# A causal mask moved from the matrix engine to zeros written by GpSimd, with a reworked residual and last gates

## The chip, the cores and the metric

The kernel runs on one core of a Trainium2 chip. Its engines work side by side, each through its own instructions in order: TensorE (PE in the profile, with PEld for its weight loads), VectorE (DVE), ScalarE (ACT), GpSimd (POOL) and SyncE (SP), which here issues the DMAs. The metric is device time in microseconds; less is better. Numbers such as 1847.95 us are medians of several runs; the profile is one further execution, recorded instruction by instruction.

## What is computed

The input is `x` with 16 sequences ("batches" below) of 512 tokens of 128 channels. Four blocks follow one another, each with `x = layernorm(x + block(x))`:

```
block 1  x = ln(x)*ln0_g + ln0_b                          # so x enters the block's own residual
         xn = ln(x)*pre_g + pre_b; xx = xn one token earlier
         k = exp(min(mix_k(xn,xx) @ Wk, 60)); v = mix_v @ Wv; r = mix_r @ Wr
         wk, wkv = recurrences over the 512 tokens of k and k*v with decay and first
         x = x + (sigmoid(r) * wkv/(wk+eps)) @ Wo
         xn = ln(x)*post_g + post_b; x = x + sigmoid(mix @ cWr) + silu(mix @ cWk) @ cWv
block 2  a tree of 255 sigmoid gates gives 256 leaf probabilities, times leaf values, times Wout
block 3  16 heads of 8 channels, rotary positions;
         scores = q k^T / sqrt(8) + causal mask; out = softmax(scores) @ v @ Wo
block 4  softmax over 16 experts, the two greatest kept as gates g[e];
         u + sum over e of g[e]*(u @ Wr[e] + br[e]) + mean of two shared experts
```

## The kernel before

Everything of a batch is held as 128 channels on the partitions by 512 tokens. For each batch `front` (line 574) does blocks 1 and 2 and the queries and keys of block 3; its four `rwkv` pieces (line 625) do the recurrence in four chunks of 128 hidden channels. The attention runs in four groups of four heads. It makes two passes over the scores. In the first, `greatest` (line 854), the scores of 128 queries stand on the partitions (`sc`), a matmul with the mask's values adds -1e30 where a key lies in the future, and VectorE takes the greatest of each row (`nmx`). These maxima are appended to the queries as further rows by a small DMA (`rows`). In the second, `weighted` (line 910), 128 keys stand on the partitions (`st`); the maxima are then subtracted by the matmul itself, ScalarE takes the exponential into a tile `e` (`ew` in the profile), and `sums` (line 940) multiplies by the values with a column of ones (`vaug`), giving the weighted sum and the denominator (`o`). `ends` (line 956) divides, multiplies by Wo and normalizes to `u`. `gating` (line 1007) computes the gates, writes them to DRAM (`gd`) and reads each pair back, spread over all partitions (`gb`, 512 KB). `by_gate` (line 1080) multiplies `u` by one gate (`us`), and `experts` (line 1094) sums 16 matmuls of `us` and one of the shared experts into `acc`.

In the second pass a group has four key tiles. Tile `kt` holds keys 128 kt to 128 kt + 127 and only the queries from 128 kt on: 512, 384, 256 and 128 of them. Only the first 128 of these queries can lie before a key, so only these columns need the mask. Before, one more matmul per score tile, with weights `mask` and the moving operand `idents` (four copies of the identity), adds the mask to them.

The residual of block 1 keeps `x1` without its mean and bias. Each time it is needed, PE recomputes it: `centre` times `x1`, plus `b0p` times `ones`, which adds the centred bias `ln0_b` in three bf16 parts.

The order of the work is made by a planner that runs when the program is built (`Plan`, line 66). Each piece of work is a Python generator that yields when it must wait for an event, a slot or an engine. The planner keeps a clock for each engine with an estimated cost for each operation, and lets the piece with the smallest due time plus slack go first when an engine is free. Slacks are set by kind of work and engine (`S_FRONT` and the others, lines 46 to 53). `PERIOD` and `LEAD` set from when in the planner's time the next batch's front may start. `SCORES` bounds the score tiles in flight, over both passes; `BANKS` are the eight PSUM banks. Slots such as `e_slots` (two places for `e`), `gb_slots` (two for gates), `us_slots` (three) and `norms` (one) hold a piece until a place is free. What the planner decides is fixed: each engine's order in the program is the order in which the pieces issued. On the chip an engine waits only for the data and places of its own next instruction.

`V` and `W` both are VectorE; `W` marks operations for which the planner adds cost when GpSimd is busy. Nearly all instructions are issued through the helper at lines 216 to 224, so the profile shows line L219 for them, and they are told apart by the names of their tiles.

Of the kernel before, what the change touches and what calls it, by code (L numbers as in the profile page):

```python
# [17 lines left out]
NT = T // 128  # L18
# [24 lines left out]
SCORES = 5  # L43
PERIOD = 100.0

S_FRONT = {"PE": -6.0, "V": -6.0, "A": 0.0, "G": -20.0}
S_RWKV = {"PE": -10.0, "V": 15.0, "A": -10.0, "G": 6.0}
S_GREATEST = {"PE": -30.0, "V": -3.0, "A": -3.0, "G": -30.0}
S_WEIGHTED = {"PE": -20.0, "A": 30.0, "G": -15.0}
S_SUMS = {"PE": 15.0}  # L50
S_ENDS = {"PE": 6.0, "V": -6.0, "A": 50.0, "G": -15.0}
S_GATE = {"PE": -20.0, "V": 6.0, "A": 6.0, "G": 0.0}
S_EXPERTS = {"PE": 20.0}
FREE = {}
LEAD = 60.0
RWKV_PACE = 5.0
EXPERT_PACE = 0.0
# [151 lines left out]
class Engine:  # L209
# [5 lines left out]
    def __getattr__(self, op):  # L215
        def issue(out, *args, **kw):
            if self.name in self.plan.last:
                with self.plan.tc.issue_after(self.plan.last[self.name].ins):
                    ins = getattr(self.engine, op)(out, *args, **kw)  # L219
            else:  # L220
                ins = getattr(self.engine, op)(out, *args, **kw)
            self.plan.did(self.name, self.cost(op, out, *args))
            self.plan.last[self.name] = ins
            return ins
        return issue
# [27 lines left out]
def pool_us(op, out, *_):  # L253
    return 0.25 + 0.0022 * columns(out)
# [3 lines left out]
def rwkv_tree_attn_moe(ctx: ExitStack, tc: tile.TileContext, a: dict, out: bass.AP):  # L258
# [35 lines left out]
    e_slots, us_slots, gb_slots = Slots(plan, 2), Slots(plan, 3), Slots(plan, 2)  # L294
# [28 lines left out]
    w_at = load("w_at", pool=p2, tag="e4")  # L323
# [44 lines left out]
    ones, b0p, minus = fixed("ones", [PARTS, T], BF16), fixed("b0p", [PARTS, D], BF16), fixed("minus", [128, 2])  # L368
    decay, first = fixed("decay", [128, NC4]), fixed("first", [128, NC4])

    def prepare_mixes():

        V.memset(ones, 1.0)
        b0 = pp.tile([128, PARTS], F32, tag="b0", name="b0")
        for i in range(PARTS):
            V.tensor_copy(b0[:, i:i + 1], col(V_LN0B))
        yield
        p = yield from bank("p_b0")
        mm(p[0:PARTS, 0:D], b0, centre, start=True, stop=True)
# [8 lines left out]
        b0r = pp.tile([PARTS, D], F32, tag="b0r", name="b0r")  # L388
        V.tensor_copy(b0r, p[0:PARTS, 0:D])
        give(p)  # L390
        b0m = pp.tile([PARTS, D], BF16, tag="b0m", name="b0m")
        for i in range(PARTS):
            V.tensor_copy(b0m, b0r)
            V.tensor_tensor(b0r, b0r, b0m, ALU.subtract)
            if i == 0:
                V.tensor_scalar(b0p, b0m, ident[0:PARTS, 0:1], None, ALU.mult)
            else:
                V.scalar_tensor_tensor(b0p, b0m, ident[0:PARTS, i:i + 1], b0p, ALU.mult, ALU.add)
# [48 lines left out]
    masks, idents = (fixed(x, [128, HG, 128], BF16) for x in ("masks", "idents"))  # L447
    mask, identb = masks[:, 0, :], idents[:, 0, :]
# [7 lines left out]
    def prepare_attention():  # L456
# [12 lines left out]
        for i in range(HG):  # L469
            copy(masks[:, i, :], mask32)  # L470
            copy(idents[:, i, :], ident)
# [85 lines left out]
    def variance(d, tag):  # L557

        sq = t512(tag)
        act(sq, d, AF.Square)  # L560
# [13 lines left out]
    def front(b, keep):  # L574
# [19 lines left out]
        def shifted_norm(p, g, minus_b, b):  # L594

            r = yield from normed(p, sq, rr)
# [3 lines left out]
            V.scalar_tensor_tensor(xn[:, 1:T + 1], p, g, r, ALU.mult, ALU.mult)  # L600
            give(p)
# [14 lines left out]
        mm(p, centre, x1, start=True, stop=False)  # L616
        mm(p, b0p, ones, start=False, stop=True)
        yield
        dx, xx, shift = yield from shifted_norm(p, col(V_PREG), minus[:, 0:1], col(V_PREB))
# [54 lines left out]
        mm(p, centre, x1, start=True, stop=False)  # L674
        mm(p, b0p, ones, start=False, stop=False)
        event("x1", b).set()
        for c in range(NC4):
            yield event("rw", b, c)
            mm(p, tm_o[:, c, :], rw[:, c, :], start=False, stop=(c == NC4 - 1))
# [510 lines left out]
```

## Time and profile before

| | us |
|---|---|
| median of 3 runs | 1847.95 (1846.07 to 1852.24) |
| the profiled execution, whole | 1852.02 |
| its span, first to last instruction | 1850.2 |

| engine | first exponential and before it | rest |
|---|---|---|
| ACT, first `ew` of the second pass | starts at 203.5 | last starts at 1784.5 |
| SP, output of the first batch | issued at 450.58 | last at 1846.98 |

Times in the profile are from the span's start. A row such as "113.4, 221" after a group's form and count gives its busy time in us and the mean length of one in ns; what follows is the idle time of the engine just before these instructions and what ended it. "out<-in" names the tile written and those read. In a table by stretches, each engine's busy time in us stands with the number of its instructions, and behind them the granted TensorE clock (1.00 is full), the busy share of the DMA engines and their GB/s. Matmuls on PE are pipelined, and each fp32 matmul of 512 columns shows as two records.

### The profile page before, as it was taken

The numbers are of one execution on the slowest core, as the hardware profiler recorded it, in microseconds if no ns is written. First come the engines' busy times: TensorE is split into PE (matmuls) and PEld (weight loads), VectorE is DVE, ScalarE is ACT, GpSimd is POOL, SyncE is SP. The second block draws the span as 40 slices with busy tenths as digits, with TensorE's granted clock in tenths as the row PEclk, the third lists the DMA queues.
The fourth block names the chain that finished last, engine by engine and source line by source line (L and its number), as shares of the span: only waits on it lengthen the run. The fifth ranks groups of instructions, "written<-read, shape, count | busy, mean of one in ns | idle before, by whom it ended". The sixth has DMA issues, their size and how long they took to land.

```text
span 1850.2 us, 25410 instructions
## 1 busy us (share of the span) xinstructions
PE 1667.9 (90%) x8580; PEld 784.5 (42%) x8668; DVE 1367.0 (74%) x1917; ACT 1172.0 (63%) x1974; POOL 1063.3 (57%) x1329
## 2 busy tenths in 40 slices
PE   5577889899999999899999999999899999998875
PEld 2233434344444444444444444444344444454431
DVE  7695879688888778686887788796878868555512
ACT  3345677668677576667767676767667666765440
POOL 2344544556765747566565757675666757545342
PEclk9687999899999999999999999999999999999996
DMA  3001010221413122222313132222213131233322
GB/s 103 1 6 56 20 38 27 79 79 32 132 37 112 62 91 78 66 82 73 97 46 105 62 96 78 95 67 65 74 58 116 51 107 62 61 94 111 97 80 97
DMA packets 61970, 133.78 MB, mean 72 GB/s; under 512 B 11708, under 2 KB 32974, under 8 KB 61585
## 3 DMA queue, kind: packets, MB, share of 16 engines
q1 hardware_dynamic: 61841, 132.16, 22.6%
q8 instruction: 69, 1.13, 0.2%
q14 instruction: 60, 0.49, 0.1%
HBM read 114.01 MB, written 17.31 MB: 71 GB/s over the span
## 4 chain that ended last, share of the span: by engine, by line
PE 49%; DVE 25%; POOL 11%; issue 6%; ACT 4%; DMA 2%; SPq 1%; POOLq 0%; DVEq 0%; ACTq 0%
PE acc L219 8%; PE sc L219 7%; PE st L219 6%; DVE sk L219 6%; PE o L219 5%; DVE skv L219 5%; PE p L219 5%; PE pv L219 4%; DVE nmx L219 3%; PE pr L219 2%; PE ph L219 2%; POOL us L219 2%; PE pk L219 2%; POOL lp L219 2%; PE pvv L219 2%
## 5 line engine op out<-in xcount | busy, mean ns | idle before, releaser
L219 DVE TENSOR_REDUCE nmx<-sc 128x1 f32<-128x384 f32 (+3 forms) x704 | 433.8, 634 | 195.6 <-PE sc L219 148.4
L219 ACT ACTIVATE ew<-st 128x512 f32<-128x512 f32 (+1 forms) x704 | 382.3, 556 | 252.1 <-PE st L219 248.0
L219 POOL TENSOR_TENSOR us<-u,gb 128x512 f32<-128x512 f32 x248 | 328.5, 1334 | 159.3 <-PE acc L219 83.6
L219 PE MATMUL acc<-us,w_mo 128*128 128x512 f32 x512 | 277.7, 634 | 17.0 <-POOL us L219 16.7
L219 PE MATMUL st<-qop,kop 128*128 128x512 bf16 (+1 forms) x1018 | 253.9, 304 | 18.1 <-DMA qop<-rows 8.5
L219 PE MATMUL sc<-kop,qop 128*128 128x128 bf16 x1021 | 257.4, 305 | 11.3 <-DVE nmx L219 7.5
L219 DVE RECIPROCAL sk<-sk 128x512 f32<-128x512 f32 x64 | 213.8, 3341 | 0.0
L219 PE MATMUL o<-ew,vaug 128*32 128x512 f32 (+3 forms) x2048 | 193.8, 447 | 6.6 <-ACT ew L219 3.4
L219 POOL TENSOR_TENSOR sk<-fk,sk 128x512 f32<-128x512 f32 x64 | 102.2, 1597 | 142.2 <-DVE sk L219 123.3
L219 PEld LDWEIGHTS <-qop 128*128 128x128 bf16 x1024 | 94.1, 100 | 182.8 <-issue 158.7
L219 PE MATMUL st<-idents,masks 128*128 128x128 bf16 (+2 forms) x673 | 161.7, 240 | 0.6 <-issue 0.4
L219 PE MATMUL sc<-masks,idents 128*128 128x128 bf16 (+2 forms) x656 | 154.9, 236 | 0.3 <-issue 0.2
L219 PEld LDWEIGHTS <-kop 128*128 128x128 bf16 x1024 | 91.6, 99 | 146.7 <-issue 102.5
L219 POOL TENSOR_TENSOR skv<-t,skv 128x512 f32<-128x512 f32 x64 | 81.4, 1272 | 89.1 <-DVE skv L219 84.3
L219 POOL TENSOR_TENSOR rw<-skv,sk 128x512 f32<-128x512 f32 x64 | 86.8, 1357 | 64.5 <-DVE sk L219 61.0
L219 PEld LDWEIGHTS acc<-us,w_mo 128*128 128x128 f32 x512 | 84.1, 195 | 80.7 <-issue 42.1
L219 POOL TENSOR_TENSOR lp<-gates,lp 128x8 f32<-128x8 f32 (+6 forms) x224 | 115.2, 536 | 2.7
L219 DVE TENSOR_TENSOR_SCAN skv<-decay,kv 128x511 f32<-128x511 f32 x64 | 112.7, 1761 | 0.0
L219 PEld LDWEIGHTS <-idents 128*128 128x128 bf16 x704 | 69.8, 99 | 88.8 <-issue 82.9
L219 PE MATMUL pv<-sq,mean_w 128*128 128x512 f32 x160 | 93.2, 666 | 14.3 <-ACT sq L219 13.5
L219 PE MATMUL p<-rw,w_tm 128*128 128x512 f32 x128 | 74.3, 664 | 34.9 <-POOL rw L219 34.5
L219 ACT ACTIVATE r<-pv,eps 128x512 f32<-128x512 f32 x96 | 65.9, 687 | 52.9 <-PE pv L219 30.1
(213 smaller groups left out, 3120.6 us busy)
## 6 DMA issues: line engine op xcount, KB each, us to landing
gb<-gd SPq DMA_DIRECT2D x128, 512.0 KB
qop<-there SPq DMA_DIRECT2D x576, 32.0 KB
kop<-there SPq DMA_DIRECT2D x192, 96.0 KB
there<-parts SPq DMA_DIRECT2D x32, 384.0 KB
x<-xT SPq DMA_DIRECT2D x16, 256.0 KB
out<-sqb SPq DMA_DIRECT2D x16, 256.0 KB
qop<-rows SPq DMA_DIRECT2D x192, 4.0 KB
w_mo<-w_mo SPq DMA_DIRECT2D x1, 1160.0 KB
```

What stands on the lines that cost most here:

```text
L219: ins = getattr(self.engine, op)(out, *args, **kw)
```

## The change

1. **Mask.** `weighted` no longer issues the mask matmul. After a tile's exponentials, GpSimd's `affine_select` goes over the first 128 queries of the tile's four heads, 128 partitions by 4 x 128, and writes 0 where the key is later than the query. Only then is the tile's event set, for which `sums` waits. `idents`, the four copies of the identity, becomes one copy `identb`; the first pass keeps its mask matmul.
2. **Places of `e`.** Instead of two places of 4 x 512 columns there is one for each key tile, sized to it: 4 x 512, 4 x 384, 4 x 256 and 4 x 128 columns, with a slot each.
3. **Residual.** `b0p` and `ones` go. After the one matmul of `centre` by `x1`, ScalarE writes the result plus the centred bias (`cb0`) back into `x1` in SBUF. The norm that follows (`shifted_norm`) reads `x1` from SBUF, on `W`. At the end of the recurrence the sum for `p2` holds the four `tm_o` matmuls alone; VectorE adds `x1` on the way into `x2`, where ScalarE copied before. `summed`, for which the next batch's front waits, is set after that addition.
4. **Last gates.** For the last batch the first six gates are loaded into the places of the exponentials of key tiles 0 and 1, which are free by then; the other ten take the two `gb` places as before. `HOLD = 16` lets the experts of the last batch but one begin only when the sixteenth (last) exponential tile of the last batch has been masked.
5. **Numbers of the planner.** `SCORES` 6 for 5, `PERIOD` 96 for 100, `LEAD` 40 for 60, other slacks and paces, and a cost for `affine_select`.

```diff
-SCORES = 5
-PERIOD = 100.0
+SCORES = 6
+PERIOD = 96.0
...
-LEAD = 60.0
-RWKV_PACE = 5.0
-EXPERT_PACE = 0.0
+LEAD = 40.0
+RWKV_PACE = 3.0
+HOLD = 16
+HOLD2 = 0
+SPLIT = 1
+EXPERT_PACE = 1.0
...
 def pool_us(op, out, *_):
-    return 0.25 + 0.0022 * columns(out)
+    return 0.25 + (0.001 if op == "affine_select" else 0.0022) * columns(out)
...
-    e_slots, us_slots, gb_slots = Slots(plan, 2), Slots(plan, 3), Slots(plan, 2)
+    e_slots, us_slots, gb_slots = [Slots(plan, 1) for _ in range(NT)], Slots(plan, 3), Slots(plan, 2)
...
-        mm(p, centre, x1, start=True, stop=False)
-        mm(p, b0p, ones, start=False, stop=True)
-        yield
-        dx, xx, shift = yield from shifted_norm(p, col(V_PREG), minus[:, 0:1], col(V_PREB))
+        mm(p, centre, x1, start=True, stop=True)
+        yield
+        act(x1, p, AF.Identity, bias=cb0)
+        give(p)
+        dx, xx, shift = yield from shifted_norm(x1, col(V_PREG), minus[:, 0:1], col(V_PREB))
...
-        mm(p, centre, x1, start=True, stop=False)
-        mm(p, b0p, ones, start=False, stop=False)
-        event("x1", b).set()
         for c in range(NC4):
             yield event("rw", b, c)
-            mm(p, tm_o[:, c, :], rw[:, c, :], start=False, stop=(c == NC4 - 1))
-        event("summed", b).set()
+            mm(p, tm_o[:, c, :], rw[:, c, :], start=(c == 0), stop=(c == NC4 - 1))
...
-        copy(x2, p)
-        dx, xx, shift = yield from shifted_norm(p, col(V_POSTG), minus[:, 1:2], col(V_POSTB))
+        V.tensor_tensor(x2, p, x1, ALU.add)
+        event("summed", b).set()
+        give(p)
+        dx, xx, shift = yield from shifted_norm(x2, col(V_POSTG), minus[:, 1:2], col(V_POSTB))
...
-                    slot_e = yield e_slots
+                    slot_e = yield e_slots[kt]
...
-                    e = p2.tile([128, HG, T], F32, tag="e4", name="ew")
+                    e = pp.tile([128, HG, n_q], F32, tag=f"e{kt}", name="ew")
...
-                               start=(i == 0), stop=False)
-                        mm(sc[:, :, 0:128], mask, idents[:, 0:per, :], start=False, stop=True)
+                               start=(i == 0), stop=(i == per - 1))
...
+                    yield
+
+                    G.affine_select(out=e[:, :, 0:128], in_=e[:, :, 0:128], pattern=[[0, HG], [1, 128]], compare_op=ALU.is_ge,
+                                    fill=0.0, base=0, channel_multiplier=-1)
...
-                slot = yield gb_slots
-                gb = p2.tile([128, 2, T], F32, tag="gb", name="gb")
+                if b == B - 1 and q < 3:
+
+                    slot = None
+                    if q % 2 == 0:
+                        yield e_slots[q // 2]
+                        past = pp.tile([128, HG, T - 128 * (q // 2)], F32, tag=f"e{q // 2}", name="gb")
...
+                else:
+                    slot = yield gb_slots
+                    gb = p2.tile([128, 2, T], F32, tag="gb", name="gb")
...
+            hold = {B - 2: HOLD, B - 3: HOLD2}.get(b, 0)
+            if hold:
+                yield event("e", B - 1, (hold - 1) // NT, (hold - 1) % NT)
             acc = yield from bank("acc")
```

## The prediction

> **What bounds it now.** I read the busy shares first, then the same by stretches, then single matmuls in order of time, then the forms of the operations that change, and last the chain that ended last.
>
> ```profile
> PE 1667.9 (90%) x8580; PEld 784.5 (42%) x8668; DVE 1367.0 (74%) x1917; ACT 1172.0 (63%) x1974; POOL 1063.3 (57%) x1329
> ```
>
> PE leads, but a share over the whole span mixes a start, a middle and a tail. The table by stretches (length, then busy time of PE, PEld, DVE, ACT, POOL, then granted clock) parts them:
>
> ```profile
> 0.00:200.00 200.00, 129.13 (x285) 53.48 (x288) 145.50 (x202) 91.08 (x136) 74.20 (x104) 0.82 0.12 38
> 350.00:1650.00 1300.00, 1249.33 (x6705) 593.75 (x6771) 1024.85 (x1404) 903.74 (x1527) 829.63 (x1038) 0.99 0.25 79
> 1786.00:1850.00 64.00, 33.26 (x81) 14.01 (x80) 14.69 (x32) 9.56 (x16) 12.84 (x9) 0.71 0.22 74
> ...
> 1150.00:1200.00 50.00, 48.23 (x245) 22.53 (x247) 34.58 (x64) 36.61 (x64) 35.46 (x40) 1.00 0.30 95
> 1200.00:1250.00 50.00, 49.44 (x276) 23.27 (x278) 47.60 (x50) 33.36 (x55) 34.99 (x44) 1.00 0.23 71
> ```
>
> The reader is to see three stages. Up to 200 us no attention runs and PE has room. From 350 to 1650 us PE is busy 96% of the time. From 1786 us on everything waits in one chain. In the middle DVE is no bystander: in the slices that hold the recurrence it is at 47.6 of 50, in those between at 34.6. In the timeline the first output is issued at 450.58 and the thirteenth at 1700.43, so a batch takes 104.1 us; DVE needs about 85 of them.
>
> **The mask's matmuls: size of the gain.** Each of 16 batches has four head groups. In the second pass a group writes 11 score tiles, each ended by a mask matmul: eight of 128 columns, two of 256, one of 512, so 704 in all.
>
> ```profile
> L219 PE MATMUL st<-idents,masks 128*128 128x128 bf16 x512 | 113.4, 221 | 0.6 <-issue 0.4
> ```
>
> and in order of time (start, duration):
>
> ```profile
> 909.28 0.22 PE L219 MATMUL sc<-masks,idents 128*128 128x128 bf16 x1
> 909.34 0.38 PE L219 MATMUL st<-qop,kop 128*128 128x512 bf16 x1
> 909.55 0.22 PE L219 MATMUL st<-idents,masks 128*128 128x128 bf16 x1
> 909.61 1.08 PE L219 MATMUL pz<-route,y 128*128 128x255 f32 x4
> ```
>
> By the row, one costs 221 ns; with 278 ns for 256 columns (row: 35.6 us) and 387 ns for 512 the sum is 113.4 + 35.6 + 64 x 0.387 = 174 us. The starts say otherwise: 909.28 to 909.34, 909.55 to 909.61. The next matmul starts 0.055 us after a mask matmul; the rest of the 221 ns is the pipe draining beside it. For 256 columns the starts are 0.11 us apart (919.75, 919.86), for 512 0.22 us (927.18, 927.40). Here the Trainium skill speaks against the row: "Perfetto Trace Analysis", section Identifying the Most-Contended Engine, says that matmul busy time is no measure of headroom, since matmuls are pipelined. By the row I would book 174 us, by the starts 64 x (8 x 0.055 + 2 x 0.11 + 0.22) = **56 us**; I take the starts. The weight loads that go with them (704 of 99 ns) lie under other matmuls and I book nothing for them.
>
> **Residual on PE.** Per batch two bias matmuls (917.37 to the next start 917.68: 0.31 us) and one of `x1` by `centre` (900.32 to 901.27: 0.95 us) go: 16 x (0.62 + 0.95) = 25 us. In all PE loses 81 us, 5.1 per batch.
>
> **What other engines get.** ACT loses the copy into `y` and gains one Identity per batch, both 128x512 and about 0.6 us: nothing. DVE gains 16 additions from PSUM at 0.67 us (row att<-z,pw): 11 us. POOL gets 256 selects over 512 columns each. Nearest rows:
>
> ```profile
> masks.py:30 POOL TENSOR_SCALAR_AFFINE_SELECT mask<-mask 128x128 f32<-128x128 f32 x1 | 0.3, 294 | 0.1
> L219 POOL TENSOR_TENSOR lp<-gates,lp 128x512 f32<-128x512 f32 x32 | 37.7, 1200 | 0.3
> L219 POOL TENSOR_TENSOR lp<-gates,lp 128x128 f32<-128x128 f32 x32 | 16.0, 523 | 0.3
> ```
>
> From 294 ns at 128 columns, 384 more cost 0.32 us at the slope of the memsets (206 ns for 128 columns, 659 for 668) and 0.68 us at that of lp: 0.62 to 0.97 us. The select reads one input, so I take 0.75, nearer the low end: 192 us (159 to 248). A rule speaks against it: "GPSIMD Engine Reference", section Engine selection, keeps elementwise work off this engine (about twice VectorE's time for two inputs, but near line rate for one), and its specifications have it share its SBUF interfaces with VectorE. The trace shows the sharing: the scan sk takes 1214 ns at best and 2061 at worst, with a mean of 1532. Over its best value it loses 20 us in 64; skv 37, the multiply-add behind it 20, the five mixes 26: 103 us of DVE beside 1063 us of POOL, 0.097 us per us of POOL. So 192 us more cost DVE about 19 us. The 32 `xn` now read SBUF twice instead of PSUM once (744 ns, never over 753); at the mixes' loss of 0.32 us that is 10 us. DVE +40 us, 2.5 per batch.
>
> **What lies on the path.** Without DVE the batch falls from 104.1 to 99.0 us. DVE then needs 88 of 99, POOL (1063 + 192)/16 = 78 of 99; neither is full over a batch. But in the recurrence slices DVE is full already, so there DVE's own +2.5 and the lost PE time meet: I give back 1.7 us per batch. 15 batch distances x (5.1 - 1.7) = **-51 us**. Before the first exponential (203.5 us) nothing is gained: PE waits there.
>
> The select adds 0.75 us and a wait in POOL's queue (a multiply of 1.27 us at most times) between the exponentials and `o`. Its cover is the places: with one per key tile a group's four tiles can all be in flight, where two large places allowed two; and PE's listed order has scores of later tiles in front of each `o`. Behind a select that waits for ACT stand the recurrence's products and the `us` multiplies; ACT is 63% busy and its exponentials mostly wait for PE, so I book nothing. A sixth score slot and the new slacks, release distance (96 for 100) and lead change only the order; I book -8 us, bounded by +30 and -40, as nothing in the trace prices them.
>
> **Tail.**
>
> ```profile
> 1812.50 3.74 DMA gb<-gd
> ...
> 1828.29 1.78 POOL us L219
> ...
> 1833.33 3.97 DMA gb<-gd
> ```
>
> From the first landing (1816.3) to the last `acc` (1841.3) 16 experts take 25 us, since two gate places make the later loads wait. PE alone needs 16 x 0.86 = 14 at full clock (0.71 was granted). In the changed order SP issues five gate loads in a row and three more behind the previous batch's output: I estimate 17 us, **-8**. SP also has one waiting gate load of batch 14 in front of the last group's `rows` loads; it needs a single `us` of batch 14, for which a place is free, so I book nothing. Batch 14's experts, held to the last exponential tile, move 17 x 0.86 = 15 us of PE work from a stretch that is 92% busy into one with half its time idle. They run at POOL's 1.27 us a gate, some 17 us, beside the 15.6 us from the last `o` (1786.4) to `pl` (1802.0); the small gating steps will meet those multiplies, say 4 us lost. **-9**.
>
> Sum against the profiled execution's 1852.0: -51 - 8 - 8 - 9 = 1776. The median of the runs is 4 us below that execution, so the forecast for the median is **1772 us**.
>
> **Rivals.**
> - PE's whole gain comes through and the shorter release distance bites: 15 x 5.1 = 77, order 40, tail 17: 1848 - 134 = 1714, with 1740 as its near end. For: DVE has 11 us spare per batch. Against: the full slices.
> - DVE, slowed by POOL, takes most of it: selects at 0.97 us and half as much contention again, give-back 4 us per batch: 15 x 1.1 + 17 = 33, so 1815. For: 47.6 of 50. Against: 34.6 in the neighbouring slice.
> - Slower: the select on the path from exponentials to `o`. Price: 0.75 + 1.27 us of POOL ahead of it, 2 us; it decides once POOL's backlog exceeds the lead of the score tiles, about 3 us of PE. If one tile in each of 64 groups' four is late by 2 us, PE loses 128 us: 1772 + 128 = 1900; if one in two groups, 1836. For: `us` multiplies come in threes (908.07, 3.74 us). Against: POOL at 79%.
> - No change: PE's 96% is drain, not work, and the order sets the pace: 1848.
>
> **Numbers.** Forecast's own case (1740 to 1800) 0.50; more gain (1700 to 1740) 0.17; DVE takes it (1800 to 1840) 0.14; no change 0.05; slower 0.14. The range 1715 to 1838 leaves out about 2 in 10. Within 0.3% (5.5 us, what a measurement tells from no change): 0.05; faster 0.81; slower 0.14.
>
> **What would show it.** Mask rows of st gone; select rows near 0.75 us; DVE's scans slightly longer; outputs issued some 100.5 us apart; the last 64 us down to about 50. Wrong if selects are over 1 us, if PE or PEld wait long for POOL ew, or if outputs stay 104 us apart.

## The result, and the profile after

The changed kernel takes **1951.5 us** (median of 4 runs, 1950.0 to 1954.43), the kernel before 1847.28 in the same comparison. The ratio is **1.0559, 95% interval 1.054 to 1.0578**: slower by 5.6%, where 1772 us and a gain of 4% were forecast. The time lies outside the range (1715 to 1838) and above the "slower" rival too (1836 to 1900). Its profiled span is 1949.0 us.

The busy shares come first, as before, with the row of granted clock in 40 slices of the span (a digit is tenths of full speed):

```profile
PE 1651.5 (85%) x7900; PEld 753.7 (39%) x7900; DVE 1371.4 (70%) x1920; ACT 1166.1 (60%) x1973; POOL 1223.7 (63%) x1585
PEclk8777897999989999999999999999999999999998
```

PE executes 680 matmuls fewer by the records (768 by the weight loads; some records of the profile before are missing), but its busy time fell by only 16 us. The clock was lower (mean 0.918, before 0.957), and a slower matmul is busy for longer: eight `o` of 512 columns take 1.07 us at full clock (from 1165.41) and 1.94 at half (from 1188.05, below). DVE, ACT and POOL are not full either: every engine has a smaller share than before except POOL. No engine is full in this sum; the time is in waiting and, for PE, in the lower clock. The table by stretches (columns as before: length, busy time of PE, PEld, DVE, ACT, POOL with counts, clock, DMA share, GB/s):

```profile
0.00:200.00 200.00, 127.72 (x263) 54.63 (x264) 140.16 (x188) 85.89 (x128) 69.41 (x93) 0.77 0.12 38
350.00:1650.00 1300.00, 1155.61 (x5682) 530.08 (x5683) 970.23 (x1315) 836.66 (x1419) 893.49 (x1150) 0.94 0.24 72
1885.00:1949.00 64.00, 44.23 (x112) 17.34 (x110) 16.12 (x32) 9.67 (x16) 28.41 (x22) 0.89 0.34 116
1150.00:1200.00 50.00, 46.02 (x216) 20.78 (x215) 35.31 (x43) 33.15 (x56) 29.51 (x49) 0.93 0.23 72
1200.00:1250.00 50.00, 42.07 (x225) 20.33 (x223) 40.60 (x60) 30.35 (x55) 41.65 (x46) 0.95 0.17 50
```

In the middle PE is busy 89% at clock 0.94, where it was 96% at 0.99. DVE, which I had called full in the recurrence slices, is at 40.6 of 50. The last 64 us are again the stretch from the last `o` to the end, and as long as before.

What PE waits for stands in the view of waits (engine and what it executes, what ended the wait, then us in all, number of waits, longest):

```profile
POOL ew L223 <- ACT ew L223: 190.7, 118, 5.0
PEld o L223 <- POOL ew L223: 106.6, 62, 4.0
PE o L223 <- POOL ew L223: 86.1, 47, 3.7
ACT sq L223 <- DVE y L223: 68.9, 16, 13.5
PE pv L223 <- ACT sq L223: 58.1, 22, 4.1
```

Two waits are new in size. `o` waits 86 us for the select, a wait that could not exist before. `pv`, the matmul that takes mean squares for a norm, waits 58 us for ScalarE's squares, where it waited 13.5 before:

```profile
PE pv L219 <- ACT sq L219: 13.5, 9, 6.8
```

The forecast named the first as what would prove it wrong ("if PE or PEld wait long for POOL ew").

The groups by form, for what was priced by the nearest row (busy us, mean ns, then idle time before):

```profile
L223 POOL TENSOR_SCALAR_AFFINE_SELECT ew<-ew 128x512 f32<-128x512 f32 x256 | 171.5, 670 | 190.7 <-ACT ew L223 190.7
L223 DVE TENSOR_TENSOR_SCAN skv<-decay,kv 128x511 f32<-128x511 f32 x64 | 100.9, 1577 | 0.0
L223 DVE TENSOR_TENSOR_SCAN sk<-decay,k 128x511 f32<-128x511 f32 x64 | 95.1, 1486 | 0.0
L223 DVE TENSOR_TENSOR s<-tab,v 128x64 f32<-128x64 f32 x32 | 35.3, 1102 | 1.1
```

A select takes 0.67 us, 171 us in all: cheaper than the 0.75 that I took. The scans became no slower; before, they stood at

```profile
L219 DVE TENSOR_TENSOR_SCAN skv<-decay,kv 128x511 f32<-128x511 f32 x64 | 112.7, 1761 | 0.0
L219 DVE TENSOR_TENSOR_SCAN sk<-decay,k 128x511 f32<-128x511 f32 x64 | 98.0, 1532 | 0.0
```

So the select's length and its load on DVE were, if anything, priced too high. What went wrong is where it stands. Here is one place of `o` in the chain of waits between 1172 and 1190 us (start, length, engine and tile):

```profile
1178.81 5.07 DVE sk L223 x2
1183.89 1.08 DVE skv L223
...
1185.07 0.76 DVE skv L223
...
1185.89 1.26 POOL skv L223
1187.15 0.26 POOL lp L223 x2
1187.41 0.60 POOL ew L223
...
1188.05 1.94 PE o L223 x8
```

and the same on three engines in the timeline (in brackets: idle time before, and who ended it), POOL and PE below ScalarE's exponential:

```profile
1182.65 0.60 ACT L223 ACTIVATE ew<-st 128x512 f32<-128x512 f32 x1 [0.42 <-PE st L223]
```
```profile
1185.89 1.26 POOL L223 TENSOR_TENSOR skv<-t,skv 128x512 f32<-128x512 f32 x1 [2.96 <-DVE skv L223]
1187.36 0.64 POOL L223 TENSOR_SCALAR_AFFINE_SELECT ew<-ew 128x512 f32<-128x512 f32 x1
```
```profile
1188.05 1.94 PE L223 MATMUL o<-ew,vaug 128*32 128x512 f32 x8 [3.66 <-POOL ew L223]
```

The exponential ended at 1183.25. POOL was idle from 1182.93 to 1185.89: its next instruction was the recurrence's product `skv`, which waited for a VectorE scan and the multiply-add after it, and these stood behind a 3.3 us reciprocal. The select, listed behind the product, began at 1187.36, four microseconds after its data were there. `o` waited for it, and PE with it for 3.66 us. The attention and the recurrence, which had shared no ordered queue between the exponential and `o`, were now tied together by POOL's.

This is the longest kind of wait, 3.66 us in nine places, 33 of the 86 us. Over all 256 selects the trace gives 1.2 us in the mean from the end of a tile's last exponential to the start of its select, over 2 us in 69 of them and 7.8 at most. Of the 304 us that these delays add up to, POOL was executing what was listed ahead in all but 59; the largest shares are 65 us of `us`, 37 of `skv` and 32 of `four`. Of the 59 idle us, 40 were spent waiting for VectorE before `skv`. So the select is late mostly because POOL works on other pieces first, and in the worst places because POOL stands still.

The time by outputs, from the first instruction: first output issued, from there to the thirteenth, from there to the end. The four kernels further down are explained with their experiments.

| | first output | 12 distances | from 13th to end |
|---|---|---|---|
| before | 450.6 | 1249.8 | 149.8 |
| changed | 487.7 | 1306.6 | 154.7 |
| changed, select over one column | 481.3 | 1288.4 | 155.4 |
| changed, no select | 481.5 | 1257.4 | 155.7 |
| before, no mask in the second pass | 446.0 | 1229.0 | 144.1 |
| changed, mask by matmul | 467.1 | 1262.7 | 142.7 |
| before with the last gates | 491.0 | 1238.7 | 133.4 |

Of the 99 us between the two profiled spans 37 are there before the first output, 57 in the middle, 5 at the end.

### The profile page after: what moved, and what is told of

It is laid out like the page before. It is cut to its first block, busy times and chain, and to the rows that moved or that the text cites. A ratio compares the mean times of both kernels' runs of the same rounds, so it can differ in the third digit from the quotient of the medians.

```text
span 1949.0 us, 24233 instructions
## 1 busy us (share of the span) xinstructions
PE 1651.5 (85%) x7900; PEld 753.7 (39%) x7900; DVE 1371.4 (70%) x1920; ACT 1166.1 (60%) x1973; POOL 1223.7 (63%) x1585
## 3 DMA queue, kind: packets, MB, share of 16 engines
q8 instruction: 63, 1.03, 0.2%
## 4 chain that ended last, share of the span: by engine, by line
PE 51%; DVE 25%; POOL 12%; issue 4%; DMA 4%; ACT 3%; SPq 1%; DVEq 0%; POOLq 0%; ACTq 0%
PE sc L223 7%; PE p L223 7%; PE acc L223 7%; DVE sk L223 6%; PE o L223 5%; DVE skv L223 5%; PE pv L223 5%; PE st L223 5%; POOL us L223 3%; DMA gb<-gd 3%; PE pk L223 3%; POOL skv L223 3%; PE ph L223 3%; PE pr L223 2%; DVE nmx L223 2%
## 5 line engine op out<-in xcount | busy, mean ns | idle before, releaser
L223 POOL TENSOR_TENSOR us<-u,gb 128x512 f32<-128x512 f32 x248 | 339.9, 1375 | 108.4 <-DMA gb<-gd 63.1
L223 POOL TENSOR_SCALAR_AFFINE_SELECT ew<-ew 128x512 f32<-128x512 f32 x256 | 171.5, 670 | 190.7 <-ACT ew L223 190.7
L223 PE MATMUL o<-ew,vaug 128*32 128x512 f32 (+3 forms) x2048 | 199.5, 464 | 86.5 <-POOL ew L223 86.1
L223 PE MATMUL sc<-kop,qop 128*128 128x128 bf16 (+3 forms) x1024 | 268.4, 317 | 1.7 <-ACT ew L223 0.8
L223 PE MATMUL st<-qop,kop 128*128 128x512 bf16 (+3 forms) x1024 | 256.4, 312 | 6.5 <-DMA qop<-rows 6.4
L223 PE MATMUL sc<-masks,identb 128*128 128x128 bf16 (+2 forms) x704 | 179.7, 255 | 0.0
L223 PE MATMUL pv<-sq,mean_w 128*128 128x512 f32 x160 | 103.9, 736 | 58.1 <-ACT sq L223 58.1
L223 POOL TENSOR_TENSOR skv<-t,skv 128x512 f32<-128x512 f32 x64 | 82.1, 1282 | 97.3 <-DVE skv L223 92.4
L223 POOL TENSOR_TENSOR sk<-fk,sk 128x512 f32<-128x512 f32 x64 | 91.4, 1428 | 52.2 <-DVE sk L223 35.2
L223 PEld LDWEIGHTS <-identb 128*128 128x128 bf16 x704 | 72.2, 103 | 98.4 <-issue 82.1
L223 PEld LDWEIGHTS o<-ew,vaug 128*32 128x32 f32 x2048 | 41.4, 109 | 173.4 <-POOL ew L223 106.6
L223 DVE TENSOR_TENSOR_SCAN skv<-decay,kv 128x511 f32<-128x511 f32 x64 | 100.9, 1577 | 0.0
L223 DVE TENSOR_TENSOR_SCAN sk<-decay,k 128x511 f32<-128x511 f32 x64 | 95.1, 1486 | 0.0
```

Of the source, the lines that this page charges most:

```text
L223: ins = getattr(self.engine, op)(*args, **kw)
```

## The experiments

Every kernel ran beside the one before, and ratios are to it, with 95% intervals. 1% is 18.5 us.

### Parts of the change

Four kernels take the change apart. The first is the changed kernel with the mask back in PE; the others add parts to the kernel before.

**Changed kernel, mask by matmul:**

```diff
-                               start=(i == 0), stop=(i == per - 1))
+                               start=(i == 0), stop=False)
+                        mm(sc[:, :, 0:128], mask, idents[:, 0:per, :], start=False, stop=True)
...
-                    G.affine_select(out=e[:, :, 0:128], in_=e[:, :, 0:128], pattern=[[0, HG], [1, 128]], compare_op=ALU.is_ge,
-                                    fill=0.0, base=0, channel_multiplier=-1)
```

> The changed kernel with the mask back as a matmul in the second pass, and no select; places, residual, last gates and the planner's numbers stay as changed. Coupling theory (the select stands in GpSimd's queue behind products that wait for VectorE's scans, so the matrix engine waits for them before each sum o, and its clock is halved after long gaps): PE's wait for POOL ew (86 us) is gone and the time falls below the kernel before, 1800 to 1845 us. Numbers theory (slacks, release distance 96, six score slots make a bad order): it stays near 1930 us or above. Residual theory (xn from SBUF, longer front): near 1930 us too.

Measured: 1873.24 us, **1.0125** (1.008 to 1.017), between the theories and in the range of none. The select in place of the matmul makes 4.3% of the changed kernel's 5.6%, some 80 us, between two kernels whose orders differ; 23 us stay without it.

**Kernel before, numbers of the planner alone:**

```diff
-SCORES = 5
-PERIOD = 100.0
+SCORES = 6
+PERIOD = 96.0
...
-LEAD = 60.0
+LEAD = 40.0
```
(with all slacks and paces of the changed kernel)

> The kernel before with the planner's numbers of the changed one alone. Coupling theory: within 1.5% of before, 1825 to 1875 us. Numbers theory: 1920 us or more. Residual theory: within 1.5% of before.

Measured: 1914.57 us, **1.0337** (1.03 to 1.0373). The same instructions in another order cost 62 us, near the 1920 that the theory of the numbers gave. The forecast had booked -8 with bounds of +30 and -40 for these numbers.

**Kernel before, select and places of e, with before's numbers:**

```diff
-                    slot_e = yield e_slots
+                    slot_e = yield e_slots[kt]
...
-                        mm(sc[:, :, 0:128], mask, idents[:, 0:per, :], start=False, stop=True)
...
+                    G.affine_select(out=e[:, :, 0:128], in_=e[:, :, 0:128], pattern=[[0, HG], [1, 128]], compare_op=ALU.is_ge,
+                                    fill=0.0, base=0, channel_multiplier=-1)
```

> The kernel before with the select on GpSimd and a place per key tile, nothing else changed (numbers, residual and last gates as before). Coupling theory: slower than before, 1900 to 1960 us, with PE's wait for POOL ew over 60 us. Numbers theory: the 56 us of mask matmuls come through in part, 1790 to 1840 us. Residual theory: likewise 1790 to 1840 us.

Measured: 1915.86 us, **1.0346** (1.031 to 1.0382). The time is in the range of the coupling theory; PE's wait for the select is not, 30.2 us where over 60 was expected:

```profile
PE o L223 <- POOL ew L223: 30.2, 22, 4.5
```

**Changed kernel with the mask by matmul and before's numbers:**

```diff
-PERIOD = 96.0
+PERIOD = 100.0
...
+                        mm(sc[:, :, 0:128], mask, idents[:, 0:per, :], start=False, stop=True)
```

> The kernel before with the reworked residual, the last gates with their hold, and the place per key tile; mask on PE, numbers as before. Coupling and numbers theories: 25 us less PE work and a shorter tail, 1800 to 1840 us. Residual theory: 1900 us or more.

Measured: 1875.98 us, **1.0138** (1.0102 to 1.0174). Residual, last gates and places bring no gain together; no theory had this time. And with them the numbers, which cost 62 us alone, change nothing (1.0125 against 1.0138). So the parts do not add up: each edit makes the planner write a new order, and the order has a price of its own.

The whole change with before's numbers (further down) takes 1.0429, so that the select in place of the matmul, with the same numbers on both sides, costs 2.9% there, 4.3% with the changed kernel's numbers and 3.5% in the kernel before.

Two more kernels part the residual from the gates; each has the places of `e` and before's numbers.

**Residual (the last gates are taken out of the kernel above):**

```diff
-HOLD = 16
+HOLD = 0
...
-                if b == B - 1 and q < 3:
```

> The kernel before with the reworked residual and the place per key tile; mask on PE, last gates and numbers as before. If the residual's 25 us of PE work come through: 1835 to 1850 us with the 18 us that replanning alone cost on average. If the longer front (one more ScalarE step before the norm, xn from SBUF) costs: 1870 to 1890 us.

**Last gates, added to the kernel before:**

```diff
+HOLD = 16
...
+                if b == B - 1 and q < 3:
+                    slot = None
+                    if q % 2 == 0:
+                        yield e_slots[q // 2]
...
+            hold = {B - 2: HOLD, B - 3: HOLD2}.get(b, 0)
```

> The kernel before with the last gates and their hold and the place per key tile; mask on PE, residual and numbers as before. If the tail's 17 us come through: 1840 to 1855 us with the 18 us of replanning. If the held experts only move the wait: 1865 to 1885 us, with the stretch from the last o to the end no shorter than 64 us.

Measured: residual 1880.12 us, **1.015** (1.0132 to 1.0168); last gates 1864.22 us, **1.0063** (1.0045 to 1.0082). The end of the kernel with the gates is 16 us shorter (133.4 against 149.8 in the table above), which it loses again earlier. The first time lies in the range for a front that costs (1870 to 1890), the second between the two expected.

### What an order is worth

How far does the planner's order alone move the time? Three kernels are the one before with one number changed by a little: 15 to 14, 100 to 101, and 0.2 to 0.21 (the planner's cost of passing data between engines). They execute the same instructions.

```diff
-S_SUMS = {"PE": 15.0}
+S_SUMS = {"PE": 14.0}
```


> The kernel before with one slack moved by one (sums on PE 15 to 14): the same instructions, another order. Order theory (the kernel before holds an unusually good order, and any replanning loses it): 1880 to 1920 us. Coupling theory alone: within 1% of before, 1830 to 1865 us.


```diff
-PERIOD = 100.0
+PERIOD = 101.0
```


> The kernel before with the release distance 101 for 100: the same instructions, another order. Order theory: 1880 to 1920 us. Coupling theory alone: within 1% of before.


```diff
-HAND_OVER = 0.2
+HAND_OVER = 0.21
```


> The kernel before with the planner's hand-over time 0.21 for 0.20: the same instructions, another order. Order theory: 1880 to 1920 us. Coupling theory alone: within 1% of before.

Measured: 1876.72 us, **1.0157** (1.0138 to 1.0175); 1864.73, **1.009** (1.0067 to 1.0112); 1860.9, **1.0065** (1.0045 to 1.0085). Three orders that nobody chose for their time cost 12 to 29 us. The given order is the fastest of the four, though none of the three is as slow as the order theory had it, 1880 or more. And the kernel with the numbers alone is a fifth order of the same instructions, at 3.4%. A difference below about 1.6% between two kernels whose orders differ therefore says nothing of the part that was changed: the residual (1.5%), the gates (0.6%) and both (1.3 to 1.4%) are inside this scatter. The select (3.5%) is outside what one number in its last digit does, but not outside what all the numbers did; what it costs has to be read where the order is kept.

### The same order with less work

To take the order out, four kernels keep it: the planner books the old cost for what is not executed, so that PE, VectorE, ScalarE and GpSimd each list their instructions as before the edit. In the first two the changed kernel's select shrinks to one column of each head, then goes.

**Select over one column:**

```diff
-    return 0.25 + (0.001 if op == "affine_select" else 0.0022) * columns(out)
+    return 0.25 + (0.001 * 512 if op == "affine_select" else 0.0022 * columns(out))
...
-                    G.affine_select(out=e[:, :, 0:128], in_=e[:, :, 0:128], pattern=[[0, HG], [1, 128]], compare_op=ALU.is_ge,
+                    G.affine_select(out=e[:, :, 0:1], in_=e[:, :, 0:1], pattern=[[0, HG], [1, 1]], compare_op=ALU.is_ge,
```


> The changed kernel with the select over one column of each head instead of 128, and the planner told its old cost, so that each engine's order is the changed kernel's to the instruction and all waits stay; most of the mask is left out. Coupling theory (the place in GpSimd's queue costs, not the length): still 1925 to 1950 us. Load theory (GpSimd's added busy time and its collisions with VectorE cost): 1860 to 1900 us.


**No select:**

```diff
-                    G.affine_select(out=e[:, :, 0:128], in_=e[:, :, 0:128], pattern=[[0, HG], [1, 128]], compare_op=ALU.is_ge,
-                                    fill=0.0, base=0, channel_multiplier=-1)
+                    plan.did("G", 0.25 + 0.001 * 512)
```


> The changed kernel without the select, while the planner still books its time: the four compute engines keep the changed kernel's order to the instruction (on SP two gate loads move by a place), but o waits for ScalarE's exponential alone. The mask of the second pass is left out. Coupling theory: most of the 80 us that one column left over goes, 1850 to 1880 us. Order theory (the listed order is poor whatever o waits for): 1915 to 1930 us, as with one column.

Measured: 1928.58 us, **1.0434** (1.0414 to 1.0454), and 1896.22 us, **1.0235** (1.0216 to 1.0253). The first is in the range of the coupling theory, the second in neither range. In the second, two gate loads change places on SP; all else is in the same order. Hence, in this order, the 0.43 us by which one column shortens the mean select are worth 1.0559 - 1.0434 = 1.25%, 23 us, and a select of 0.24 us that stands in POOL's queue 1.0434 - 1.0235 = 2%, 37 us. The pair does not part two ways of standing there: `o` waits for POOL, and what POOL has listed behind the select waits for ScalarE's exponential (190.7 us above). POOL's busy time with one column is 1107.7 us, 116 less than in the changed kernel, and still PE waits for the select:

```profile
L223 POOL TENSOR_SCALAR_AFFINE_SELECT ew<-ew 128x4 f32<-128x4 f32 x256 | 62.1, 243 | 226.9 <-ACT ew L223 225.5 <-DMA qop<-there 1.0
PE o L223 <- POOL ew L223: 64.0, 41, 3.2
```

With no select this wait is gone, and that of `pv` has grown; the kernel is 43 us slower than before although PE has the work of the mask and of the residual less:

```profile
PE pv L223 <- ACT sq L223: 81.6, 21, 5.9
```

The other two frozen kernels ask what a microsecond less is worth to the kernel before: on PE (its second pass without mask matmuls) and on VectorE (a multiply in place of the recurrence's reciprocal).

**Before, no mask in the second pass:**

```diff
-                        mm(sc[:, :, 0:128], mask, idents[:, 0:per, :], start=False, stop=True)
+                        plan.did("PE", tensor_us("matmul", sc[:, :, 0:128], mask, idents[:, 0:per, :]))
```


> The kernel before without the mask matmuls of the second pass (the mask is left out there), every engine's order otherwise frozen to the instruction. PE-bound theory (the forecast's): 1790 to 1805 us, 45 to 56 us less. Chain theory (the time is set by waits that cross engines in the frozen order, VectorE's above all, and PE has slack that its busy share hides): 1830 to 1850 us.


**Before, a shorter step in place of the reciprocal:**

```diff
+    R = Engine(plan, "V", nc.vector, lambda op, out, *_: vector_us("reciprocal", out))
...
-            V.reciprocal(sk, sk)
+            R.tensor_scalar(sk, sk, 0.0, None, ALU.mult)
```


> The kernel before with the recurrence's reciprocal (3.34 us, 64 times) replaced by a multiplication by zero of under 1 us, every engine's order frozen; the division is left out. PE-bound theory: 1835 to 1850 us, as VectorE is not the bound. Chain theory: 1700 to 1790 us, since at least 60 of the 150 us and more that VectorE loses come through.

Measured: 1820.88 us, **0.9851** (0.9826 to 0.9876), 28 us less, for the 56 us of mask matmuls; 1832.84 us, **0.9905** (0.9886 to 0.9924), 18 us less, for 167 us of VectorE (busy 1199.8 against 1367.0). The first lies between the ranges of the two theories, the second 2 us below that of the PE-bound one. So about half of what PE was relieved of came through, and a tenth of VectorE's. PE was the engine nearest to a bound, as read, but not the bound. Its stretch in the middle, without the mask:

```profile
350.00:1650.00 1300.00, 1223.67 (x6302) 567.98 (x6355) 1034.92 (x1427) 915.15 (x1557) 847.35 (x1053) 0.99 0.26 80
```

94% busy where it was 96%: the freed time went partly into waits.

### Other orders of the changed kernel

If the select comes late because `o` is listed too close behind it, the planner should list `o` later when it is told that a masked tile is ready 4 us later than it thinks.

```diff
-                    event("e", b, g, kt).set()
+                    plan.go(plan.end + LATER, masked(b, g, kt))
```


> The changed kernel with its select, the planner told that a masked tile is ready 4 us later than it books, so that each o is listed later on the matrix engine. Coupling theory: PE has other work in front of o while the select waits, PE's waits for POOL ew shrink and the time falls to 1880 to 1925 us. Order theory: anything within the spread that replanning gives, 1930 to 1970 us, with the waits for POOL ew gone or not.

Measured: 1947.54 us, **1.051** (1.0476 to 1.0543). This misses the 1880 to 1925 that the coupling theory gave and is what the order theory gave (1930 to 1970). PE's wait for the select is gone all the same:

```profile
PE o L224 <- POOL ew L224: 1.5, 2, 1.2
```

So 86 us of waits can go without the time following. The experiment also writes a new order, and POOL still waits 164 us for the exponentials in front of its selects; which of the two takes the time was not isolated. The wait of `o` is a sign of the select's cost in the order in which it is seen, not its measure.

What is the second wait, of `pv` for ScalarE's squares? The timeline has it in every period of 112.6 us. VectorE first, then POOL, ScalarE and PE:

```profile
1240.61 1.22 DVE L223 TENSOR_TENSOR m<-m,tab 128x64 f32<-128x64 f32 x1
...
1242.12 1.79 DVE L223 TENSOR_TENSOR s<-tab,v 128x64 f32<-128x64 f32 x1
...
1244.34 0.68 DVE L223 TENSOR_TENSOR y<-p,x 128x512 f32<-128x512 f32 x1
```
```profile
1240.46 1.28 POOL L223 TENSOR_TENSOR us<-u,gb 128x512 f32<-128x512 f32 x1
1241.70 2.13 POOL L223 TENSOR_TENSOR four<-four,parts 128x1024 f32<-128x1024 f32 x1
```
```profile
1245.06 0.63 ACT L223 ACTIVATE sq<-y 128x512 f32<-128x512 f32 x1 [4.07 <-DVE y L223]
```
```profile
1245.74 2.08 PE L223 MATMUL pv<-sq,mean_w 128*128 128x512 f32 x2 [3.68 <-ACT sq L223]
```

`y<-p,x` is the residual's new addition. Before, ScalarE copied and squared straight from PSUM, and VectorE had no part between `p` and `pv`. Now the addition stands in VectorE's queue behind nineteen small steps of `gating` and a few others, from 1234.03 on. PE had ended the sum `p` at about 1232.8 (timeline: the last two matmuls of `p<-rw,w_tm` from 1231.74, 1.02 us); the addition began 11.6 us later. Most of the small steps take 0.18 to 0.3 us, but those that meet a POOL instruction take longer: the two shown last until it ends (1241.83 beside 1241.74; 1243.91 beside 1243.83), 1.22 and 1.79.

Four more kernels are the whole change in another order: gating with a greater slack on VectorE (25 for 6), all of before's numbers, the cost of passing data 0.21, and a release distance of 80.

```diff
+S_GATING = {"PE": -3.0, "V": 25.0, "A": 50.0, "G": -6.0}
...
-                         (greatest, S_GREATEST), (weighted, S_WEIGHTED), (sums, S_SUMS), (ends, S_ENDS), (gating, S_ENDS),
+                         (greatest, S_GREATEST), (weighted, S_WEIGHTED), (sums, S_SUMS), (ends, S_ENDS), (gating, S_GATING),
```


> The changed kernel with the gating steps given a later due time on VectorE (25 for 6), so that other work there goes first. Hole theory (the addition into x2 stands behind some 20 small gating steps, which collide with GpSimd): PE's waits for ACT sq before pv fall from 58 us to under 25 us and the time to 1890 to 1925 us. Select theory (what is lost is lost to the select in every order): 1940 us or more.


```diff
-SCORES = 6
-PERIOD = 96.0
+SCORES = 5
+PERIOD = 100.0
...
-LEAD = 40.0
+LEAD = 60.0
```
(and all other slacks and paces of before)

> The whole change with the planner's numbers of the kernel before. Order theory (this listed order was unlucky): 1880 to 1920 us. Select theory: 1925 to 1960 us.


```diff
-HAND_OVER = 0.2
+HAND_OVER = 0.21
```


> The changed kernel with the planner's hand-over time 0.21 for 0.20: the same instructions in another order. Order theory: anywhere from 1880 to 1950 us, and lower than 1940 us. Select theory: 1940 to 1970 us.


```diff
-PERIOD = 96.0
+PERIOD = 80.0
```


> The changed kernel with fronts released every 80 instead of 96, so that the planner is never held back by the release and its order need not repeat from batch to batch. Order theory: 1880 to 1930 us, the outputs no longer exactly 112.5 us apart. Select theory: 1935 us or more.

| whole change, order by | us | ratio (95%) | PE `pv` waits for ACT `sq` | PE `o` waits for POOL `ew` |
|---|---|---|---|---|
| its own numbers | 1951.5 | 1.0559 (1.054 to 1.0578) | 58.1 | 86.1 |
| gating later | 1908.33 | 1.0307 (1.0278 to 1.0335) | 34.0 | 60.6 |
| before's numbers | 1930.45 | 1.0429 (1.0377 to 1.048) | 18.5 | 40.1 |
| passing data 0.21 | 1913.01 | 1.0332 (1.031 to 1.0353) | 16.4 | 45.7 |
| release distance 80 | 1923.48 | 1.0391 (1.0367 to 1.0416) | 19.0 | 56.3 |

Two of the rows behind the table, of the kernel with 0.21:

```profile
PE o L223 <- POOL ew L223: 45.7, 35, 4.4
...
PE pv L223 <- ACT sq L223: 16.4, 15, 1.9
```

All four are faster than the changed kernel's own order, and slower than the kernel before in its given order and the three next to it (1.0157 at most), though not all slower than it is with the changed kernel's numbers (1.0337). With `o` listed later, six orders of the changed kernel lie between 1.031 and 1.056, with a mean of 1.0421; five of the kernel before lie between 1 and 1.034, with a mean of 1.0130. **By these means the change costs 2.9%, about 54 us, and its own order another 1.4%, about 26 us, above its mean.** The two ranges overlap and the orders were not drawn at random, so this is a rough figure; it agrees with the 3.2% of the select in the frozen order and with the 2.9 to 4.3% of the pairs with the same numbers. The wait of `pv` is the mark of the changed kernel's own order: it shrinks in all others. But it does not set their times (gating later has the longest in the table after the first row, 34.0 where under 25 was expected, and is the fastest), and that it is the cause of the 26 us was not isolated. The wait of `o` for the select is in all five of the table.

No kernel that computes the whole function was faster than the one before.

## Why the prediction was wrong, step by step

**The step that failed: the select was held to be covered, and for POOL's queue the sum has "ACT is 63% busy and its exponentials mostly wait for PE, so I book nothing."** Ahead of a select it saw one multiply of 1.27 us, covered by the places and by PE's listed order; for what stands behind it, nothing. Ahead stand other pieces of work, `us`, `four` and the recurrence's products, and the products wait for VectorE; so an exponential that is done waits for them, at worst for a scan of another piece, and `o` with it. The delay was over 2 us in 69 of 256 places, and PE's order did not cover it in 47 (86 us). Behind, POOL itself waited 190.7 us for ScalarE in front of the selects. In the changed kernel's order, kept instruction by instruction, the select costs 60 us: 23 of length, 37 of standing there. The rival "slower: the select on the path" named the place and, at 2 us late, the size of the delay, but took "POOL at 79%" as evidence against. POOL was 63% busy, and its next instruction was late all the same, for the most part with work listed ahead and in the worst places idle (`skv` waited 92.4 us for VectorE in 49 waits). The occupancy of a queue does not tell how late its next instruction is. Part of the 60 us can be the clock: TensorE was at half speed for 147 us between 400 and 1600 us, for 92 with the select gone, so the clock can make up to 27 us of the difference; the forecast of the middle has no term for it (last section).

**What else is in the 104 us.** The changed kernel without its select is still 43 us slower than before, in the same order and with 81 us less for PE. At the half that came through for the mask, 40 of these 81 us should have been seen (an estimate from the kernel before without its masks); so some 80 us lie in the order, the residual, the places and the gates. They were not parted, the places of `e` were never run alone, and what the 80 us are made of stays open.

**The bound: half right.** The mask matmuls' 56 us, by the starts, were meant to come through less a give-back of a third. In the same order they are worth 28 us (23 to 32). PE at 96% in the middle was read as a bound, and the rival "no change" as nearly excluded; the truth lies between the two. By the row's 174 us it would have been further off still.

**The residual: one term mis-sized, one missed.** On VectorE it was 11 us of length, "nothing" on ScalarE. The addition's place was not priced: it puts VectorE's queue between `p` and `pv`, where there had been PSUM and ScalarE only. In the changed kernel's order this stood behind gating, and `pv` waited 58 us for 13.5; in the other orders of the table it waited 16 to 34, and 16.0 with the mask by matmul, so the price hangs on the order. Residual and places cost 1.5% together, within the scatter of orders: the 25 us of PE were not seen, and a loss by the residual is not shown.

**VectorE: +40 us forecast, +4 measured** (1371.4 against 1367.0). The 19 us of contention with more POOL work did not show in the scans' means (1486 and 1577 ns, before 1532 and 1761). Nor did they show in the same order with less POOL work: with one column POOL is busy 116 us less, for which the forecast's 0.097 would give 11 us of VectorE, and VectorE is busy 1.6 us less (1369.8). The 0.097 was read as a price per microsecond of POOL; how much two engines hinder each other depends on which instructions meet, and this the edits change too.

**The planner's numbers: -8, bounds +30 and -40.** Alone they cost 62 us, with residual and gates nothing. The bound was too narrow: a change of one number in the last digit moves the kernel before by 12 to 29 us. Every part of the change came with a new order, and this term was booked once, with a gain, for no row of the trace.

**The start.** "Before the first exponential nothing is gained" was right for a gain; the loss was not thought of. 37 of the 99 us are there at the first output, and 31 of them without any select (481.5 against 450.6). The kernel before with the last gates, which has neither select nor new residual, stands at 491.0 there, so a new order can do this alone.

**The end: -17 forecast, +5 measured from the thirteenth output on.** The gates come as forecast; the timeline shows five loads in one go on SP and `acc` for ten experts without a pause between:

```profile
1913.95 2.60 SPq L1068 DMA_DIRECT2D gb<-gd  x5
```
```profile
1919.85 10.92 PE L223 MATMUL acc<-us,w_mo 128*128 128x512 f32 x20 [4.06 <-POOL us L223]
```

In the order with the gates alone the end is 16 us shorter, close to the sum of both terms, though other orders without these gates end in 143.0 to 151.6 us where the given one takes 149.8. In the changed kernel the gain is given back: the end is 155 us with the select and also without it (155.7), so the select's own wait is not what takes it. With the mask by matmul, in another order, it is 142.7. What takes it in the changed order stays open.

**What was right:** the length of a select (0.67 for 0.75), that POOL is not full over the span (63%), that the starts come nearer to a mask matmul's worth than the busy row, and one of the signs of a wrong forecast, PE waiting for POOL `ew`. The outputs were neither 100.5 us apart nor 104: 112.6 in the middle, 108.9 in the mean of twelve distances.

Open, too, is why one order of the same instructions is 12 to 62 us slower than another; the traces show different waits, and no run isolated one of them.

## What to carry to other kernels

When a step moves to another engine, read what is listed ahead of it in that engine's queue and what those instructions wait for; an engine with an ordered queue can be late without being full, and the step ties together two chains that were independent. Where a planner fixes the order, first measure how far the order alone moves the time (here 0.65 to 1.6% for one number in the last digit, 3.4% for all the numbers); a difference within that says nothing of the change, and one of a pair with a frozen order speaks of the change in that order. A frozen order with the work taken out also tells before any rewriting what an engine's time is worth: here a microsecond of PE was worth half a microsecond, one of VectorE a tenth.

## What the runs showed of the hardware that had not been expected

A pause of PE of 3.7 us costs more than its length. In the wait that ended at 1188.05 the granted clock fell to 0.5, by the clock records from 1186.77 to 1193.60, and eight matmuls of `o` took 1.94 us for 1.07. Around the wait that ended at 1245.74 it was the same again, from 1244.79 to 1251.62. The pause of 1.93 us between them, which ended at 1217.06, had no such stretch. In the table by stretches the granted clock stands third from the end:

```profile
1188.05:1193.55 5.50, 5.50 (x19) 2.07 (x20) 2.45 (x2) 0.75 (x2) 4.40 (x11) 0.50 0.00 0
1217.06:1222.56 5.50, 5.50 (x41) 2.70 (x42) 3.18 (x4) 3.96 (x6) 5.27 (x9) 1.00 0.01 2
```

In the changed kernel's trace all 20 pauses of 3.5 us or more between 400 and 1600 us came with a stretch at 0.5, and none of the 44 of 0.5 to 2 us. TensorE was at half speed for 147 us of these 1200 us, for 24 us before. As PE does half the work there, this bounds the clock's own part in the 1200 us at (147 - 24)/2, about 62 us, if it had been busy all that time; how much of it was on the path was not measured. In the traces of the kernels with a select the time at half speed is 78 to 147 us, with the mask by matmul 14 to 41, and 92 in the changed kernel with its select left out.

A small VectorE step with two SBUF inputs that begins inside a POOL instruction lasted until that instruction ended: 1.79 us for a step that takes 0.22 alone (`s<-tab,v`, mean 1.10 over 32 in the changed kernel, 0.49 before). In the changed kernel's trace this holds for all 58 steps of gating that began so with at least 0.25 us of the POOL instruction to run: each ended within 0.15 us of its end. The 53 single-input reductions in the same place kept their 0.22.
